# Gated projections with eight columns innermost: PSUM read with a step, SBUF written in order

## The chip, the core and the metric

The kernel runs on one core of a Trainium2 chip. The metric is device time in microseconds of one execution; the median of several runs counts. A profiled execution leaves a trace with the start and the duration of each engine's instructions. The engines are TensorE (PE; its weight loads are PEld), VectorE (DVE), ScalarE (ACT), GpSimd (POOL) and SyncE (SP), which issues DMAs. TensorE's results land in PSUM; the other memory on the core is SBUF.

## The reference, cut to what matters

Four layers run one after the other on an image batch of 4 x 128 x 128 x 128 floats, each as x + layer(group norm of x): a deformable convolution, a scan of 1-D convolutions over rows, a layer of summed messages, and a triangle layer. The change lies in the last one:

```python
xn = layer_norm(x, norm_g, norm_b)
left = xn @ left_w + left_b
right = xn @ right_w + right_b
left = left * jax.nn.sigmoid(xn @ lgate_w + lgate_b)
right = right * jax.nn.sigmoid(xn @ rgate_w + rgate_b)
out_gate = jax.nn.sigmoid(xn @ ogate_w + ogate_b)
out = jnp.einsum('bkjd,bkid->bijd', left, right)
out = layer_norm(out, onorm_g, onorm_b) * out_gate
return out @ to_out_w + to_out_b
```

## The kernel before, in words

The deformable convolution fills the span to about 3350 us and the scan to about 4100 us. The last two layers are one function, `message_and_triangle` (L1175). It takes the four images of the batch one at a time (b). One image lives in SBUF as X: 128 partitions by 128 columns by 128 floats.

For an image, `sums_of` builds X from the messages (products on TensorE at L1354, VectorE at L1365, squares on ScalarE at L1372). `turned` scales X (L1459), transposes it (L1469), copies it back (L1470) and counts its moments (L1476). `spread` applies the layer norm (L1494), transposes back (L1503, L1504), and computes the output gate (L1509, L1513), which it stores. These work on groups of 32 columns (g = 0 to 3), in blocks of 4 columns.

`projected` computes left and right with their gates for one quarter q of the 128 hidden channels (DQ = 32). A block covers QB = 8 columns. Eight matmuls (L1534, 16 records each block in the profile, as each matmul has two) fill a PSUM tile `proj_ps` of 8 columns by QC = 128 results: 32 of left, 32 of right, 32 of each gate. One sigmoid on ScalarE (L1538) turns the 64 gates of the 8 columns into the SBUF tile `work`. Two products on VectorE (L1540), one for left and one for right, multiply PSUM with `work` and write into L and R. L and R are laid out as partitions by channel by column, so that `triangle` (L1552, copied out by ScalarE at L1556) can take one channel's 128 columns as a matrix. PSUM holds each column's results side by side, so neighbouring columns of one channel lie 128 floats (512 bytes) apart in PSUM and side by side in L and R.

`proj_ps` has two buffers (pool `l3ps_q`), shared with `self_ps`; `work` has two too. A buffer of `proj_ps` is free for TensorE again when the second product, into R, has read it.

The order on each engine is written out by hand: `weave` interleaves lists of steps by their counts, and all five engines run in the order in which the steps were issued. For each image: five rounds (g = 0 to 4) that weave `turned` of group g+1, `spread` of group g and `projected` of quarters 0 and 1 for group g-1; the last of these rounds has projections alone. Then the triangle of quarter 0; then quarters 2 and 3, each woven with the triangle of the quarter before (two blocks of projections and one of triangle in turn), the last with small steps for the next image; then the triangle of quarter 3; then the moments of the result (L1567) and the output (`given`: L1595 and L1600 norm, L1610 transpose, L1612, L1613, L1620, L1624, L1627), woven with the next image's `sums_of` and `turned`.

Other lines that the prediction uses as measures: L509 (VectorE, 390 elements from PSUM and SBUF in order), L551 (VectorE, PSUM and SBUF in order), L507 and L530 (ScalarE copies from PSUM, L530 in runs of four floats), L1068 (ScalarE, PSUM in order), and the scan's VectorE lines, among them L1119 and L1127 (in order), L1128 (SBUF read at every third float) and L1145 (PSUM read and SBUF written at every third float).

Of the kernel before, what the change touches and what calls it, by code (L numbers as in the profile page):

```python
# [9 lines left out]
F32 = mybir.dt.float32  # L10
I32 = mybir.dt.int32
BF16 = mybir.dt.bfloat16
AF = mybir.ActivationFunctionType
ALU = mybir.AluOpType
# [4 lines left out]
P = 128  # L19
# [13 lines left out]
DQ = P // NQ  # L33
# [1141 lines left out]
def message_and_triangle(tc, c, x2T, x3d, gates, counted, w2, w3, out):  # L1175
# [3 lines left out]
    nc = tc.nc  # L1179
# [7 lines left out]
    QB = 8  # L1187
# [3 lines left out]
    with ExitStack() as ctx:  # L1191
# [25 lines left out]
        with tc.tile_pool(name="l3prep", bufs=1) as prep, tc.tile_pool(  # L1217
            name="l3ps_w", bufs=2, space=PSUM
# [38 lines left out]
        two = ctx.enter_context(tc.tile_pool(name="l3two", bufs=2))  # L1257
# [268 lines left out]
        def projected(b, q, j_from, j_to):  # L1526

            cols = slice(q * QC, (q + 1) * QC)
            ds = slice(q * DQ, (q + 1) * DQ)

            def block(j0):
                pp = ps_q.tile([P, QB, QC], F32, name="proj_ps", tag="ps_q")
                for j in range(QB):
                    nc.tensor.matmul(  # L1534
                        pp[:, j], lhsT=X[:, j0 + j, :], rhs=wcat[:, cols], start=True, stop=True
                    )
                sig = two.tile([P, QB, 2 * DQ], F32, name="work", tag="work")
                nc.scalar.activation(sig, pp[:, :, 2 * DQ :], AF.Sigmoid)  # L1538
                for n, to in enumerate((L[:, ds], R[q % 2])):
                    nc.vector.tensor_tensor(  # L1540
                        to[:, :, j0 : j0 + QB].rearrange("p d j -> p j d"),
                        pp[:, :, n * DQ : (n + 1) * DQ], sig[:, :, n * DQ : (n + 1) * DQ], ALU.mult,
                    )

            return [lambda j0=j0: block(j0) for j0 in range(j_from, j_to, QB)]
# [216 lines left out]
```

## Time and profile before

| | |
|---|---|
| median of 3 runs | 5691.27 us (5687.96 to 5703.16) |
| profiled execution | 5688.34 us, span 5686.6 us |
| busy: PE, PEld | 5214.1 us (92%), 4461.0 us (78%) |
| busy: DVE, ACT, POOL | 3277.2 us (58%), 2798.5 us (49%), 780.3 us (14%) |
| matmuls of L1534 | 4096 records, 488.9 us busy |
| sigmoids of L1538 | 256, 151.1 us |
| products of L1540 | 256 into L (154.6 us), 256 into R (152.7 us) |
| mean granted TensorE clock | 0.964 |

The projections run between 4219 and 5570 us of the span, in four stretches, one for each image. A group's row gives line, engine, operation, output and inputs, shapes and count; then the busy time in us and the mean duration of one in ns; then the idle time of the engine just before these instructions and what ended it. A row of the chain of waits gives start, duration and what was running; "issue" is time in which the engine waited for nothing that the profile shows. A mean duration is longer than the distance between two instructions of one engine that follow each other without a wait[...].

### The profile page before, as it was taken

To read this page: it belongs to the slowest core of one execution; us is meant where nothing else is said; L and a number is where in the kernel's file an instruction comes from. 1 tells how busy PE (TensorE), PEld (TensorE's weight loads), DVE (VectorE), ACT (ScalarE), POOL (GpSimd) and SP (SyncE) were. 2 spreads that over 40 slices of the span, in tenths; PEclk is the share of its full clock that TensorE was granted. 3 is DMA by queue.
4 is the path that set the end of the run, shared out by engine and by line. 5 is a ranking of instruction groups with operands and counts; after the bars stand their busy time and mean duration, and the time that the engine had idled before them with its cause. 6 is when DMAs were issued, how large, how long until landed. Compare 5 with 4: busy or idle time off the path is not lost. (4 is left out here: it accounts for less than half of the span.)

```text
span 5686.6 us, 112077 instructions
## 1 busy us (share of the span) xinstructions
PE 5214.1 (92%) x42401; PEld 4461.0 (78%) x42401; DVE 3277.2 (58%) x10323; ACT 2798.5 (49%) x5890; POOL 780.3 (14%) x674
## 2 busy tenths in 40 slices
PE   2899999999999999999999979999879788798897
PEld 1778888888888888888888879999848568577686
DVE  5544444554444544445433359999974764756756
ACT  1355554455554455555544423333264673764746
POOL 2021211001110011111000002222100200200202
PEclk9899999999999999999999989999989999999999
DMA  4555555556554555555443422222230531623515
GB/s 145 139 138 133 137 125 114 132 123 137 133 137 99 128 135 127 138 120 126 101 82 68 80 60 90 90 90 90 78 150 31 204 145 43 232 90 112 213 42 169
DMA packets 1132346, 671.45 MB, mean 118 GB/s; under 512 B 736461, under 2 KB 1002894, under 8 KB 1113366
## 3 DMA queue, kind: packets, MB, share of 16 engines
q1 hardware_dynamic: 1121650, 657.77, 43.6%
q8 instruction: 338, 5.54, 0.4%
q10 hardware_dynamic: 10148, 6.43, 0.4%
q14 instruction: 210, 1.72, 0.1%
HBM read 382.88 MB, written 281.11 MB: 117 GB/s over the span
## 5 line engine op out<-in xcount | busy, mean ns | idle before, releaser
L509 DVE TENSOR_TENSOR m<-ty,t_ps 120x390 f32<-120x390 f32 x1548 | 804.6, 557 | 1501.6 <-ACT ty L507 1500.4
L520 PEld LDWEIGHTS v_ps<-m,pixels 120*128 120x128 f32 x11352 | 1440.4, 194 | 86.0 <-issue 8.9
L520 PE MATMUL v_ps<-m,pixels 120*128 120x108 f32 (+1 forms) x11352 | 1466.3, 274 | 3.6 <-ACT v L530 3.5
L530 ACT COPY v<-v_ps 128x432 f32<-128x432 f32 x1376 | 718.9, 522 | 1275.8 <-PE v_ps L520 1272.8
L578 PE MATMUL conv_ps<-v,wdef 128*128 128x128 f32 (+2 forms) x5160 | 1304.0, 379 | 6.4 <-DVE x1c L551 5.9
L578 PEld LDWEIGHTS conv_ps<-v,wdef 128*128 128x128 f32 x5160 | 814.6, 193 | 255.8 <-issue 21.4
L507 ACT COPY ty<-t_ps 120x390 f32<-120x390 f32 x1560 | 688.1, 489 | 176.7 <-PE t_ps L497 169.2
L497 PE MATMUL t_ps<-places,spread 25*120 25x99 bf16 (+1 forms) x10836 | 520.4, 260 | 61.1 <-DVE m L509 36.5
L497 PEld LDWEIGHTS <-spread 25*120 25x120 bf16 x10896 | 339.3, 137 | 222.9 <-issue 121.5
L1534 PEld LDWEIGHTS proj_ps<-wcat,X 128*128 128x128 f32 x4096 | 480.2, 194 | 30.0 <-issue 29.0
L1534 PE MATMUL proj_ps<-wcat,X 128*128 128x128 f32 x4096 | 488.9, 278 | 1.7 <-DVE R L1540 0.4
L392 POOL TENSOR_TENSOR off<-off,koff 72x512 f32<-72x512 f32 x128 | 162.0, 1266 | 2295.5 <-DVE off L389 2202.7
L1540 DVE TENSOR_TENSOR L<-proj_ps,work 128x256 f32<-128x256 f32 x256 | 154.6, 604 | 384.8 <-ACT work L1538 384.8
L1068 ACT ACTIVATE rowT<-x1T_ps,t_x,s_x 128x128 f32<-128x128 f32 x512 | 192.7, 457 | 367.5 <-PE x1T_ps L1061 347.2
L1081 PE MATMUL m_ps<-carry,w 128*128 128x172 f32 x2286 | 361.7, 311 | 0.0
L1613 POOL TENSOR_TENSOR work<-work,gate 128x512 f32<-128x512 f32 x128 | 164.2, 1283 | 1417.6 <-ACT work L1612 1165.3
L1081 PEld LDWEIGHTS m_ps<-carry,w 128*128 128x128 f32 x2286 | 346.0, 188 | 0.0
L1148 POOL TENSOR_TENSOR sum_h<-sum_h,x2c 128x512 f32<-128x512 f32 x128 | 162.3, 1268 | 1166.7 <-DVE x2c L1145 1166.7
L1538 ACT ACTIVATE work<-proj_ps 128x512 f32<-128x512 f32 x256 | 151.1, 597 | 311.1 <-PE proj_ps L1534 311.1
L1624 PE MATMUL out_ps<-outw,work 128*128 128x128 f32 x1024 | 193.8, 292 | 34.1 <-POOL work L1613 33.5
L1354 PE MATMUL self_ps<-R,ws 128*128 128x512 f32 x256 | 157.6, 705 | 70.1 <-DVE X L1365 60.9
L1624 PEld LDWEIGHTS out_ps<-outw,work 128*128 128x128 f32 x1024 | 164.8, 203 | 46.8 <-POOL work L1613 46.8
(231 smaller groups left out, 6635.5 us busy)
## 6 DMA issues: line engine op xcount, KB each, us to landing
pixels<-tab SPq DMA_DIRECT2D x688, 123.8 KB
xin<-in_x_dram SPq DMA_DIRECT2D x56, 1024.0 KB
off<-parts SPq DMA_DIRECT2D x64, 891.0 KB
tab<-rows SPq DMA_DIRECT2D x384, 128.0 KB
places<-off SPq DMA_DIRECT2D x688, 55.7 KB
x<-x1c SPq DMA_DIRECT2D x32, 1024.0 KB
x1rows<-x SPq DMA_DIRECT2D x128, 256.0 KB
x2T<-x2c SPq DMA_DIRECT2D x128, 256.0 KB
```

Source lines behind the costliest of these rows:

```text
L497: nc.tensor.matmul(to, lhsT=spread[p0 : p0 + KROWS, ph, :], rhs=mov, start=True, stop=True,)
L507: nc.scalar.copy(ty[:, 0:n], tp[0:LANES, 0, 0:n])
L509: nc.vector.tensor_tensor(m, ty[:, 0:n].rearrange("p (r c) -> p r c", c=PADW), tx, ALU.mult)
L520: nc.tensor.matmul(vp[:, h * n : h * n + rows * w].rearrange("p (k c) -> p k c", c=w), lhsT=pix[0:LANES, xb, :], rhs=m[:, :, RX * xb : RX ...
L530: nc.scalar.copy(v[:, :, c0 : c0 + 4 * RX].rearrange("p k (h c) -> p k h c", c=RX), vp[:, 0 : 4 * n].rearrange("p (h k c) -> p k h c", h=4 ...
L578: nc.tensor.matmul(pc[:, at : at + r1 - r0, :], lhsT=wdef[:, 3 * ky + kx, :], rhs=v[:, k0 + kx, r0:r1, kx : kx + S], start=m == 0, stop=m ...
L1068: nc.scalar.activation(rt[:, b, :], px[:, b, :], AF.Identity, bias=t, scale=s)
L1081: nc.tensor.matmul(to, lhsT=wgt, rhs=src[:, :, at : at + n], start=i == 0, stop=i + 1 == len(todo),)
L1148: nc.gpsimd.tensor_tensor(sum_h, sum_h, x2c[:, :, i], add)
L1534: nc.tensor.matmul(pp[:, j], lhsT=X[:, j0 + j, :], rhs=wcat[:, cols], start=True, stop=True)
L1613: nc.gpsimd.tensor_tensor(a, a, gt, ALU.mult)
L1624: nc.tensor.matmul(po[:, j], lhsT=a[:, j], rhs=outw, start=False, stop=True)
```

## The change

Sigmoid and products go through the same elements in another order: channels outside, the eight columns innermost. `work` becomes channel by column in place of column by channel. The sigmoid and the products read PSUM with a step of 512 bytes between neighbours in the order of work; the products read `work` and write L and R in that order, in L and R as runs of eight floats. Before, they read PSUM in order and wrote L and R with a step of 512 bytes. Nothing else differs: the matmuls, the sizes of all tiles, the number of instructions and their order on each engine, and the waits are those of before.

```diff
-                sig = two.tile([P, QB, 2 * DQ], F32, name="work", tag="work")
-                nc.scalar.activation(sig, pp[:, :, 2 * DQ :], AF.Sigmoid)
+                sig = two.tile([P, 2 * DQ, QB], F32, name="work", tag="work")
+                nc.scalar.activation(
+                    sig, pp[:, :, 2 * DQ :].rearrange("p j n -> p n j"), AF.Sigmoid
+                )
                 for n, to in enumerate((L[:, ds], R[q % 2])):
+                    es = slice(n * DQ, (n + 1) * DQ)
                     nc.vector.tensor_tensor(
-                        to[:, :, j0 : j0 + QB].rearrange("p d j -> p j d"),
-                        pp[:, :, n * DQ : (n + 1) * DQ], sig[:, :, n * DQ : (n + 1) * DQ], ALU.mult,
+                        to[:, :, j0 : j0 + QB], pp[:, :, es].rearrange("p j d -> p d j"),
+                        sig[:, es], ALU.mult,
                     )
```

## The prediction

> **What bounds the kernel now.** I read the page first (busy times, costliest groups), then the groups by shape, then the timeline and the chain of waits over the stretch in which the projections run (4219 to 5570 us). By the page TensorE is busy 92% of the span, VectorE 58%, ScalarE 49%; what matters is where the two wait on the changed lines' chain. From the groups by shape (columns: count, then busy us and mean ns of one, then idle before):
>
> ```profile
> L1540 DVE TENSOR_TENSOR L<-proj_ps,work 128x256 f32<-128x256 f32 x256 | 154.6, 604 | 384.8 <-ACT work L1538 384.8
> ...
> L1567 DVE BATCH_NORM_STATS2 stats_o<-L 128x6 f32<-128x128 f32 x512 | 152.5, 361 | 33.0 <-ACT L L1556 33.0
> L1538 ACT ACTIVATE work<-proj_ps 128x512 f32<-128x512 f32 x256 | 151.1, 597 | 311.1 <-PE proj_ps L1534 311.1
> ...
> L1595 ACT ACTIVATE normed<-L,off_o,r_o 128x128 f32<-128x128 f32 x256 | 143.7, 612 | 3.1 <-DVE off_o L1446 3.1
> ...
> L1476 DVE BATCH_NORM_STATS2 stats_x<-X 128x6 f32<-128x128 f32 x512 | 110.6, 279 | 33.3 <-ACT X L1470 33.2
> ...
> L551 DVE SCALAR_TENSOR_TENSOR x1c<-conv_ps,xres 128x256 f32<-128x256 f32 x16 | 6.6, 415 | 0.0
> ```
>
> The reader is to see that a product of 256 elements that writes with a step of 512 bytes takes 604 ns, where a DVE operation of the same size with everything in order takes 415 (L551). The step costs 189 ns, 0.74 ns an element. Reading SBUF at that step costs much the same: 361 against 279 for 128 elements (L1567, L1476), 0.64 each. VectorE waits for the sigmoid before nearly every block, so sigmoid and products are one chain behind TensorE. Whether that chain sets the end differs by stage. Timeline where only projections are left (end of a batch's first two quarters):
>
> ```profile
> 4329.48 0.60 ACT L1538 ACTIVATE work<-proj_ps 128x512 f32<-128x512 f32 x1 [1.19 <-PE proj_ps L1534]
> ...
> 4330.11 0.61 DVE L1540 TENSOR_TENSOR L<-proj_ps,work 128x256 f32<-128x256 f32 x1 [0.75 <-ACT work L1538]
> 4330.56 0.60 DVE L1540 TENSOR_TENSOR R<-proj_ps,work 128x256 f32<-128x256 f32 x1
> ...
> 4331.61 0.60 ACT L1538 ACTIVATE work<-proj_ps 128x512 f32<-128x512 f32 x1 [1.54 <-PE proj_ps L1534]
> ```
>
> L and R start 0.45 us apart, so sigmoid to the end of R is 4329.48 to 4331.16: 1.68 us. There the chain shows two blocks every 3.92 us (pieces of 3.81 to 3.83 and 0.12 of issue), against 3.57 to 3.59 elsewhere: both PSUM buffers are held by the sigmoid and the products. In the stage with triangles a pair of blocks and a triangle take 4.47 us throughout; a buffer is free there at 4351.07 and wanted at 4351.81, so 0.74 us of slack hides the chain. In the stage that still turns X, the chain of waits is:
>
> ```profile
> 4238.10 3.59 PE proj_ps L1534 x32
> 4241.68 0.02 issue
> 4241.70 0.45 ACT work L1538
> 4242.15 0.04 issue
> 4242.20 0.40 ACT X L1459
> ```
>
> Only the sigmoid of the second block is on it; ScalarE's next work queues behind. One stage later (nothing left to turn), it goes on through VectorE:
>
> ```profile
> 4304.81 0.61 ACT work L1538
> 4305.41 0.02 issue
> 4305.44 0.59 DVE L L1540
> 4306.03 0.43 DVE R L1540
> 4306.46 0.18 DVE normed L1494
> 4306.64 0.14 issue
> 4306.78 1.01 PE back_ps L1503 x4
> ```
>
> Adding up all pieces of the chain from 4219 to 5570 us, L1538 is on it 53 times (29.6 us) and the products 80 times (40 of L, 40 of R; 39.7 us). The change can move only these and the 3.92 us loop.
>
> **The change part by part.** No instruction is added, removed or moved: every queue, SP's and POOL's included, holds the same instructions in the same order, with the same waits. Matmuls, DMAs, tile sizes and what L and R hold are the same. Three kinds of access change.
>
> Products, write side: runs of 8 floats (32 bytes) in place of single floats 512 bytes apart. Nearest row: ScalarE's square at L1372 reads SBUF in runs of four at that step, 512 elements in 721 ns, no dearer than L1459's 821 for 512 in order. I take the write as free: 604 goes to 415. The sigmoid's output and the products' second input stay in order: nothing.
>
> Products, read side: PSUM with a step of 512 bytes. No row has this step. Nearest is the scan's L1145, which reads PSUM and writes SBUF one float in three, 12 bytes apart, 172 elements in 378 ns; L1119, both in order, takes 336. So 42 ns for both sides together, 0.24 ns an element at most. Lower bound 0: reading SBUF at 12 bytes alone costs L1128 395 against L1127's 328 at 168 elements, 0.40 each, so the write can explain all of L1145. Upper bound, if PSUM behaves as SBUF: 0.64, which makes the product 415 + 164 = 579. I take 0, as L1145 is the only PSUM row with single floats and leaves little for the read. Below nothing is excluded: the read is in order now.
>
> Sigmoid, read side: the same step, 512 elements, ScalarE at 0.81 ns each (L1612's 769 for 512 less L1068's 457 for 128, over 384). The nearest ScalarE row is L530, PSUM in runs of four: 522 ns for 432, where L507's 489 for 390 plus 42 x 0.81 gives 523, so nothing; but it has no single floats. If L1145's whole 0.24 is the read, a float comes every 1.04 + 0.24 = 1.28 ns, and ScalarE pays 0.47 each, 0.24 us. If it is all the write, PSUM still only shows that it keeps VectorE's 1.04, and ScalarE pays at most 0.23 each, 0.12 us. The far end is the SBUF price: L1595 reads single floats at 512 bytes, 128 in 612 ns; L1068 does the same arithmetic from PSUM in order in 457, and SBUF as source adds 52 (821 of L1459 less 769 of L1612), so 103 ns for 128, 0.80 each, 0.41 us. I take 0.06 us, half of 0.12, and keep 0 to 0.41.
>
> Here a rule speaks against the change. The Trainium skill, "Advanced Engine Details and Errata", Memory Cachelines, says PSUM has lines of 8 bytes, wants every two consecutive elements to be neighbours, and warns that non-contiguous access slows matmuls; for SBUF it states a penalty for a new 16-byte line at every access. Charged on every float here at the SBUF rows' price, it makes the sigmoid 1.01 us and the product 579 ns. But L1145 at 12 bytes already meets a new 8-byte line at every float, and shows at most 0.24. By the row the sum is a gain, by the rule a loss (below). I go with the row.
>
> Sum. Back to back, the products now start 0.445 us apart; in order they should start 0.445 - 0.111 = 0.334 apart (L509's pairs: two of 390 in 1.03 us, 557 each, so 0.473 apart, 1.04 x 390 + 67, with 1.04 ns an element from L551's 549 for 384 and 415 for 256; for 256 this is 0.334). On the chain each pair is followed in VectorE's own queue, so it saves 2 x 0.11 = 0.22: 40 x 0.22 = 8.9 us. The loop: L's start to R's end shrinks from 1.05 to 0.334 + 0.415 = 0.75, by 0.30, and 3.92 falls to near TensorE's 3.59: 0.33 x 3 pairs x 4 batches = 4.0. Together 12.9. What is late next: in the stages with norm, ScalarE's copies and TensorE's gate product end soon after, at the end of a group ScalarE's two table loads (1.28 us each); I give a fifth back: 10.3. The sigmoid costs 53 x 0.06 = 3.2. Net 7.1 us. Products with triangles stay behind TensorE: zero, and that cover is 0.74 us, which would be gone only if sigmoid and products together grew by more.
>
> The profiled execution took 5688.3 (span 5686.6), the median of the runs is 5691.3, 2.9 higher. 5691.3 - 7.1 = 5684.2, so 5684.
>
> **The rivals.** *PSUM at SBUF's price* ends slower. Sigmoid +0.41 on 53 chain places: 21.8 us. Products 579 ns, but starting 0.334 + 0.164 = 0.498 apart, 0.05 more than now: 80 x 0.05 = 4.2. Loop +0.41 + 0.03 = 0.44, x 12 = 5.3. Sum 31: 5722. For it: the rule, and the SBUF rows agreeing on two engines (0.64 and 0.80). Against it: L1145. It decides once the sigmoid grows by 10.3/53 = 0.19 us with the products' gain kept, and passes 0.3% only at about 0.52 us, or 0.3 if the products gain nothing.
>
> *The step in between*, L1145's 42 ns all the read's: product 476 ns, starts 0.395 apart, 40 x 0.10 = 4 saved; loop 0.18 saved against 0.24 lost, near zero; sigmoid 53 x 0.24 = 12.7. Net 9 slower: 5700, within 0.3%.
>
> *Hidden anyway*: the products do get shorter, but a neighbour of equal length ends 0.1 us later, so nothing arrives: 5691. For it: the saving comes in pieces of 0.2 us in 40 places.
>
> *More than counted*: sigmoid free, nothing given back, and places where the chain passes just beside VectorE gain too: 12.9 plus a third, 17: 5674 or less.
>
> *Dearer yet*:[...] if that costs beyond 0.8 ns each, the 0.74 us with triangles goes as well: over 5730. No row shows it.
>
> **How the numbers follow.** About 0.3%, 17 us, is what a measurement of this kernel can tell from no change. Likeliest, 5684: 0.37, its own range 5676 to 5692. Hidden 0.10, in between 0.08: these three are within 0.3%, 0.55. SBUF's price 0.22 and dearer yet 0.08: slower, 0.30. More than counted: faster, 0.15. The range runs from 5672 to 5724: it takes in SBUF's price and leaves out the dearer case and half of the larger gain.
>
> **What would show each step.** L1540 at about 415 ns, pairs 0.33 apart: the write was the cost and the PSUM read is free; near 480 or 580 it is one of the rivals. L1538 at 600 to 700 is my case, about 1010 the rule's. The projection-only loop should fall from 3.92 to about 3.6 us a pair, the triangle stage keep 4.47. I am wrong if L1538 gains more than 0.2 us, or if products shorten as said while waits of TensorE for ScalarE (L1470, L1504, L1513) grow by the same amount.

## The result and the profile after

| | before | after |
|---|---|---|
| median of 5 runs | 5695.07 us (5687.96 to 5703.16) | 5665.21 us (5661.05 to 5667.66) |
| profiled execution, its span | 5688.34, 5686.6 us | 5661.53, 5659.8 us |
| DVE busy | 3277.2 us | 3206.4 us |
| mean granted TensorE clock | 0.964 | 0.966 |

The section ahead of the prediction had three runs of before; here it is five. The ratio is 0.9947, with a 95% interval of 0.9932 to 0.9961: 30 us less, beyond the 0.3% that the prediction named as measurable. 7 us had been forecast, and the time lies below the range.

The groups of instructions of the changed kernel (its sigmoid is still L1538, its products are L1543):

```profile
L1538 ACT ACTIVATE work<-proj_ps 128x512 f32<-128x512 f32 x256 | 151.1, 597 | 300.0 <-PE proj_ps L1534 300.0
...
L1543 DVE TENSOR_TENSOR L<-proj_ps,work 128x256 f32<-128x256 f32 x256 | 108.4, 424 | 425.8 <-ACT work L1538 425.8
...
L1543 DVE TENSOR_TENSOR R<-proj_ps,work 128x256 f32<-128x256 f32 x256 | 105.8, 413 | 0.0
```

The sigmoid takes 597 ns as before, to the nanosecond; the products take 424 and 413 where they took 604 and 596. So a PSUM read with a step of 512 bytes costs neither engine anything here. In the loop where only projections are left, the timeline of after shows:

```profile
4321.79 0.60 ACT L1538 ACTIVATE work<-proj_ps 128x512 f32<-128x512 f32 x1 [1.26 <-PE proj_ps L1534]
...
4324.20 0.42 DVE L1543 TENSOR_TENSOR L<-proj_ps,work 128x256 f32<-128x256 f32 x1 [1.03 <-ACT work L1538]
4324.55 0.41 DVE L1543 TENSOR_TENSOR R<-proj_ps,work 128x256 f32<-128x256 f32 x1
4325.43 0.60 ACT L1538 ACTIVATE work<-proj_ps 128x512 f32<-128x512 f32 x1 [1.26 <-PE proj_ps L1534]
```

L and R start 0.35 us apart (0.45 before), and a pair of blocks takes 3.64 us (3.92 before).

**Where the time came from.** Measured from the first projection to the last triangle of each image, the four stretches of projections take 859.2 us before and 831.6 after: 27.7 us less. Everything outside them took the same in this pair (4827.4 and 4828.2). The 27.7 us can be split, because many stages run at the full granted clock in both profiles, or in the experiments below:

| stage, at full clock | before | after | for four images |
|---|---|---|---|
| rounds 1 to 3 (turn, norm, projections), an image | 98.93 us | 96.03 us | -11.6 us |
| last round (projections alone), with the first triangle and the gap behind it | 22.95 | 21.78 | -4.7 |
| quarter 2 with triangles | 35.73 | 35.73 | 0 |
| quarter 3 with triangles and small steps, images 0 to 2 | 47.40 | 45.98 | -4.2 |
| quarter 3 of image 3, no small steps | 37.98 | 37.42 | -0.6 |

(Before's quarter 3 at full clock is from the fourth experiment, its third round from the tenth.) That is 21.1 us of shorter waits, called the direct part below. The other 6.6 us are stretches at half clock: in quarter 3, before lost 7.8 us to them (48.97, 52.06 and 48.96 us less 47.40 each) and after 1.5 (one of three took 47.52), and in the rounds both lost about 10.

**The half clock.** The trace records the clock that TensorE is granted; it is 1.00 or 0.50 of full speed throughout. The chain of waits in quarter 3 of image 0, first before, then after, goes from a pair of products through small steps on VectorE to the same small product of the next image and the 16 matmuls queued behind it:

```profile
4390.73 0.59 DVE L L1540
4391.32 0.43 DVE R L1540
4391.74 0.04 DVE m_x L1285
...
4392.40 0.38 PE gn_ps L1291 x2
4392.79 3.13 PE proj_ps L1534 x16
4395.92 1.28 PE tri_ps L1552 x8
```

```profile
4383.67 0.42 DVE L L1543
4384.09 0.33 DVE R L1543
4384.42 0.08 DVE m_x L1285
...
4385.12 0.38 PE gn_ps L1291 x2
4385.51 1.89 PE proj_ps L1534 x16
4387.40 0.89 PE tri_ps L1555 x8
```

The same 16 matmuls take 3.13 and 1.89 us. Windows of 3.41 us of before, aligned to its clock record (columns: us; busy time and count of PE, PEld, DVE, ACT, POOL; granted clock; DMA), show what went ahead of it:

```profile
4389.79:4393.20 3.41, 1.02 (x9) 0.83 (x9) 1.50 (x6) 0.60 (x1) 0.00 (x0) 1.00 0.00 0
4393.20:4396.61 3.41, 3.41 (x19) 3.41 (x18) 0.00 (x0) 0.60 (x1) 0.00 (x0) 0.50 0.00 0
```

In one slot TensorE was busy for 1.02 us, since it waited 2.39 us for VectorE ahead of L1291; in the next its clock was 0.50. After the change that wait is 2.17 us and falls into two slots, in which TensorE was busy for 2.75 and 1.91 us; the clock stayed full:

```profile
4380.20:4383.61 3.41, 2.75 (x25) 2.56 (x23) 0.76 (x2) 1.75 (x3) 0.00 (x0) 1.00 0.00 0
4383.61:4387.03 3.42, 1.91 (x17) 1.91 (x18) 1.30 (x6) 0.03 (x1) 0.00 (x0) 1.00 0.00 0
4387.03:4390.44 3.41, 3.41 (x33) 3.41 (x32) 0.75 (x2) 1.46 (x3) 0.00 (x0) 1.00 0.02 5
```

So at this place it is as much the position of the slots as the shorter wait that spared the half clock. What shorter waits do on the average is counted over all profiles further down.

### The profile page after: what moved, and what is told of

It reads as the page before. It is cut to its first block, busy times and chain, and to the rows that moved or that the text cites. A ratio compares the mean times of both kernels' runs of the same rounds, so it can differ in the third digit from the quotient of the medians.

```text
span 5659.8 us, 112077 instructions
## 1 busy us (share of the span) xinstructions
PE 5198.7 (92%) x42401; PEld 4450.7 (79%) x42401; DVE 3206.4 (57%) x10323; ACT 2796.7 (49%) x5890; POOL 780.2 (14%) x674
## 5 line engine op out<-in xcount | busy, mean ns | idle before, releaser
L1543 DVE TENSOR_TENSOR L<-proj_ps,work 128x256 f32<-128x256 f32 x256 | 108.4, 424 | 425.8 <-ACT work L1538 425.8
L1538 ACT ACTIVATE work<-proj_ps 128x512 f32<-128x512 f32 x256 | 151.1, 597 | 300.0 <-PE proj_ps L1534 300.0
```

## The experiments

Each ratio is to runs of the kernel before in the same set, on the same chip. Medians of before in the three sets (experiments 1 to 4, 5 to 8 and 9 to 11) are 5695.91, 5698.27 and 5695.30 us. My theory after the result was: (1) the sigmoid costs nothing; (2) more pairs of products are on the path than I had counted, above all where the chain of waits of before names ScalarE; (3) shorter waits of TensorE spare half-clock slots. Two rivals: that the gain is spread evenly over all pairs of products, and that the clock makes most of it and the direct part is about as small as forecast.

**1 to 3: one part of the work alone.** Each kernel chooses the order by quarter and keeps the old one elsewhere; the first has the condition shown, the second `q == 2`, the third `q == 3`:

```diff
+                if q < 2:
+                    sig = two.tile([P, 2 * DQ, QB], F32, name="work", tag="work")
...
+                else:
+                    sig = two.tile([P, QB, 2 * DQ], F32, name="work", tag="work")
...
```

Quarters 0 and 1 (the rounds):

> The new order in quarters 0 and 1 alone, the old one in 2 and 3. My theory now (the shorter products count wherever TensorE waits behind a pair in VectorE's queue, and shorter idle times of TensorE leave fewer stretches at half clock): 16 to 18 us faster than before, of which 4 in the projection-only loop. Rival, a gain that is spread evenly over the products (half of them are changed here): 15 us. Rival, only the 40 places counted on the chain of waits: about 10 us.

Measured: 5666.11 us, ratio 0.995 (0.9936 to 0.9964), 30 us less by the medians, which is more than the theory and both rivals expected; its profiled execution is 20 us below that of before, with 841.0 us in the projections, 18.2 less. The stages at full clock account for 16.3 (11.6 and 4.7, as in the table); the rest of the 30 us is not placed.

Quarter 2:

> The new order in quarter 2 alone, where triangles are woven in and TensorE hides the products. My theory: no change, within 3 us of before, the stage at 35.7 us for each image as before. Rival, a gain spread evenly over the products (a quarter is changed): 7.5 us faster.

Measured: 5698.32 us, ratio 1.0003 (0.9995 to 1.001). Quarter 2 took 35.73 us in all four images, as before and after. A gain spread evenly over all pairs would have shown here; that rival falls. With triangles the products are hidden, as predicted.

Quarter 3:

> The new order in quarter 3 alone, where small steps for the next image are woven in. My theory: about 11 us faster, some 5 to 6 of it fewer stretches at half clock behind the waits for those steps. Rival, spread evenly: 7.5 us. Rival, the counted chain alone (12 pairs at 0.22): 3 us.

Measured: 5686.43 us, ratio 0.9986 (0.9977 to 0.9996), 8 to 9.5 us less. In the profile quarter 3 took 47.84, 49.42, 47.90 and 37.72 us, 5.1 less in all than before. The chain of before has five pairs there in each of the first three images, and one pair in the last: at the forecast 0.22 us that is 3.5 (the expectation had counted 12). The 5 to 6 us that the theory expected from the clock did not come: four slots ran at half clock in these quarters, five in before's. By the medians the three parts add up to 39 us, the whole change to 30; their intervals are wide enough for that, so the stages and not these medians say what each part is worth.

**4: before, with spare matmuls in the waits of quarter 3.** Three products of 256 columns go ahead of each of the three small products of the next image (L1291, L1310, L1322), into PSUM columns that nobody reads. Nothing else of before is changed:

```diff
+        def busy(to, n):
+            for _ in range(n):
+                nc.tensor.matmul(
+                    to[:, 256:512], lhsT=c.gmean, rhs=wcat[:, 0:256], start=True, stop=True
+                )
...
-                v["ps"] = small_ps([P, 1], "gn_ps4")
+                wide = small_ps([P, 512], "gn_ps4")
+                v["ps"] = wide[:, 0:1]
+                if b:
+                    busy(wide, 3)
```

> The kernel before, with TensorE kept busy in its three waits for the next image's small steps in quarter 3 (three spare products of 256 columns each, about 1.3 us, into columns of PSUM that nobody reads; images 1 to 3). The products on VectorE are the old ones. My theory, in which half clock follows from TensorE's idle time in the 3.4 us before: the half-clock stretches of quarter 3 go away (5 in the profile before), 5 to 8 us faster. Rival, in which the half-clock stretches have another cause: no change, or up to 4 us slower by the spare products.

Measured: 5680.21 us, ratio 0.9974 (0.9967 to 0.9982), 15 us less, above what was expected. Quarter 3 of image 1, windows of before and then of this kernel:

```profile
4760.20:4812.30 52.10, 43.27 (x335) 42.17 (x333) 20.78 (x53) 17.47 (x28) 0.00 (x0) 0.90 0.06 19
```

```profile
4750.10:4797.60 47.50, 42.52 (x353) 40.47 (x352) 20.80 (x53) 17.47 (x28) 0.00 (x0) 1.00 0.07 23
```

18 more matmul records, VectorE and ScalarE with the same work, and 4.6 us less: the granted clock went from 0.90 to 1.00. Over three images quarter 3 lost 7.8 us with its products at 605 and 597 ns. So the clock's part is shown without any shorter product. The rest of the 15 us is not placed: the profile differs by 11 us before the first projection, where the two kernels are the same and this one happened to spend 225 us at half clock, before 246.

**5: after, with the sigmoid in two instructions**, so that L could start when its half of the gates is there:

```diff
-                nc.scalar.activation(
-                    sig, pp[:, :, 2 * DQ :].rearrange("p j n -> p n j"), AF.Sigmoid
-                )
+                for n in range(2):
+                    gs = slice((2 + n) * DQ, (3 + n) * DQ)
+                    nc.scalar.activation(
+                        sig[:, n * DQ : (n + 1) * DQ],
+                        pp[:, :, gs].rearrange("p j n -> p n j"), AF.Sigmoid,
+                    )
```

> The changed kernel with the sigmoid in two instructions, the 256 gates of left first, then those of right. ScalarE's work grows by about 0.05 to 0.1 us a block, but VectorE's first product can start about 0.2 us earlier. If in the rounds that still turn X TensorE waits for VectorE's norm behind the products (my reading of the changed kernel's trace), these rounds get about 0.2 us shorter each, quarter 3 about 1 us an image, and the whole 10 to 15 us faster than the changed kernel. Rival, the recorded chain, in which ScalarE's queue behind the sigmoid holds those rounds: they get 0.05 to 0.1 us longer, and the whole is 0 to 3 us from the changed kernel.

Measured: 5679.48 us, ratio 0.9965 (0.9953 to 0.9978), 10 to 15 us slower than after (0.9939 to 0.9947) by the ratios. A miss. Its timeline shows why:

```profile
4230.41 0.66 ACT L1540 ACTIVATE work<-proj_ps 128x256 f32<-128x256 f32 x2 [0.76 <-PE proj_ps L1534]
4231.10 0.42 DVE L1546 TENSOR_TENSOR L<-proj_ps,work 128x256 f32<-128x256 f32 x1 [1.97 <-ACT work L1540]
```

The second half ends at 4231.07, and L starts 0.03 us later: it waited for both. The trace's semaphores say why: the first half raises none, the second raises the one that L waits for, in all 256 pairs. So the edit did not do what it was for; it only made the sigmoid 0.06 us longer. All of it arrived: rounds 1 to 3 took 0.06 us more a pair of blocks (8.03 to 8.09, 9.82 to 9.88), the last loop 3.70 for 3.64. That is the price of a sigmoid of 0.66 us which my prediction had feared. And quarter 3 took 49.33, 49.56 and 51.07 us, with seven slots at half clock where after has one. The rounds came out as the rival had said, but since L never started earlier, this run cannot tell the two readings apart.

**6: after, with each product in two of 16 channels**, which lengthens VectorE's part and nothing else:

```diff
+                    for h in range(2):
+                        hs = slice(h * DQ // 2, (h + 1) * DQ // 2)
+                        es = slice(n * DQ + h * DQ // 2, n * DQ + (h + 1) * DQ // 2)
...
-                            to[:, :, j0 : j0 + QB], pp[:, :, es].rearrange("p j d -> p d j"),
+                            to[:, hs, j0 : j0 + QB], pp[:, :, es].rearrange("p j d -> p d j"),
```

> The changed kernel with each product in two instructions of 16 channels: same access, but four starts of about 0.2 us each in place of two of 0.334, so a pair holds VectorE about 0.13 us longer, more than half of the 0.22 that the change took away. My theory: 10 to 16 us slower than the changed kernel, each clean round 0.13 us longer per pair on VectorE's path. Rival, only the 40 counted places and the loop: 6 to 7 us slower.

Measured: 5674.05 us, ratio 0.9959 (0.9943 to 0.9975), 7 to 11 us slower than after by the ratios, 9.8 us by the projections of the profiles: between the two forecasts. The single pairs tell more. The last loop went from 3.64 to 3.77 us a pair, by 0.13. The pairs of rounds which the chain of before had put down to ScalarE's gate (L1513) grew by the same 0.13: 8.03 to 8.16 and 9.82 to 9.95. VectorE sets the end there too, and now the chain of waits itself, at the place where before's went down ScalarE (shown in the next section), names VectorE's queue all the way:

```profile
4243.43 0.61 ACT work L1538
...
4244.06 0.49 DVE L L1545 x2
4244.54 0.40 DVE R L1545 x2
4244.94 0.78 DVE stats_x L1476 x4
4245.72 0.26 DVE normed L1494
...
4246.12 1.00 PE back_ps L1503 x4
```

Quarter 3 took 46.42 us three times, with no half-clock slot although its waits are longer than after's: whether a wait costs a slot also depends on where the slots begin.

**7: the products of after with the sigmoid of before.** PSUM is read with a step and L and R are written in order, but `work` stays column by column, so that the products read it with a step of 256 bytes in SBUF:

```diff
-                sig = two.tile([P, 2 * DQ, QB], F32, name="work", tag="work")
-                nc.scalar.activation(
-                    sig, pp[:, :, 2 * DQ :].rearrange("p j n -> p n j"), AF.Sigmoid
-                )
+                sig = two.tile([P, QB, 2 * DQ], F32, name="work", tag="work")
+                nc.scalar.activation(sig, pp[:, :, 2 * DQ :], AF.Sigmoid)
...
-                        sig[:, es], ALU.mult,
+                        sig[:, :, es].rearrange("p j d -> p d j"), ALU.mult,
```

> One half of the change alone: the products write L and R in order and read PSUM with the step, but the sigmoid keeps its old order, so the products read their second input from SBUF with a step of 256 bytes. If a stepped SBUF read costs 0.64 ns an element beside the PSUM read, the product takes about 580 ns and the time is that of before or up to 12 us slower. Rival, the step costs on the write alone: 415 to 425 ns and the time of the changed kernel.

Measured: 5712.32 us, ratio 1.0029 (1.0016 to 1.0042), 14 us slower than before by the medians, a little over the 12 expected at most. From its groups of instructions:

```profile
L1541 DVE TENSOR_TENSOR L<-proj_ps,work 128x256 f32<-128x256 f32 x256 | 152.5, 596 | 389.5 <-ACT work L1538 389.5
L1538 ACT ACTIVATE work<-proj_ps 128x512 f32<-128x512 f32 x256 | 151.2, 597 | 321.4 <-PE proj_ps L1534 245.2 <-DVE R L1541 76.2
L1541 DVE TENSOR_TENSOR R<-proj_ps,work 128x256 f32<-128x256 f32 x256 | 150.7, 589 | 0.0
```

The products are back at 596 and 589 ns: by its duration a product pays as much for the step on the reading side of SBUF as on the writing side; in PSUM it pays nothing. The gain of the change hangs on the sigmoid's new order. The products are 8 ns shorter than before's, and yet rounds and loop are longer (8.39 for 8.25, 3.99 for 3.93 us). The timeline of the loop shows why a mean duration is not enough:

```profile
4333.46 0.60 DVE L1541 TENSOR_TENSOR L<-proj_ps,work 128x256 f32<-128x256 f32 x1 [1.09 <-ACT work L1538]
4333.98 0.59 DVE L1541 TENSOR_TENSOR R<-proj_ps,work 128x256 f32<-128x256 f32 x1
```

R starts 0.52 us after L; over all pairs the median is 0.51 us, against 0.45 before and 0.34 after. A product thus holds VectorE 0.17 us longer with the stepped read and 0.11 us longer with the stepped write. The 0.06 us between them is the loop's loss, and two of them most of the 0.14 in the rounds. Half-clock time in the projections is 88.7 us, against 47.8.

**8: after, with the spare matmuls of the fourth kernel.**

> The changed kernel with the same spare products on TensorE in quarter 3. Fewer half-clock stretches are left there to remove (one in the changed kernel's profile): 1 to 5 us faster than the changed kernel, quarter 3 at 46.0 us in each of the first three images. Rival, in which the filled waits are not what lowers the clock: no difference, or up to 4 us slower.

Measured: 5659.53 us, ratio 0.9931 (0.9916 to 0.9947). That is 5 to 9 us below after by the ratios (1 to 5 were expected), but the intervals overlap. Quarter 3 took 45.98, 45.99 and 45.98 us without a half-clock slot. With the same matmuls added on both sides, quarter 3 differs from the fourth kernel by 1.41 us an image: the direct part alone.

**9 to 11: after once more, and before and after with spare matmuls in the rounds too.** The last two kernels add to the fourth's edit, ahead of the first two transposes and the first transpose back of g = 3, into PSUM that these then overwrite:

```diff
+                if g == 3 and k < 2:
+                    nc.tensor.matmul(
+                        pt[:, k:], lhsT=c.gmean, rhs=wcat[:, 0 : (JB - k) * S],
+                        start=True, stop=True,
+                    )
...
+                if g == 3 and k == 0:
+                    for _ in range(2):
+                        nc.tensor.matmul(
+                            pb, lhsT=c.gmean, rhs=wcat[:, 0:512], start=True, stop=True
+                        )
```

> The changed kernel once more, beside the next two on the same chip: 30 us faster than before as at first; anything from 22 to 36, since the half-clock stretches fall differently in every execution.

> The kernel before with spare products on TensorE in all its long waits among the projections: the three of quarter 3, and the starts of the last two rounds that still turn or norm (0.65 to 1.7 us each, into PSUM columns that the real product overwrites). My theory: hardly a half-clock stretch is left between the first and the last projection of an image; 12 to 18 us faster than before, with the products still at 604 ns. Rival: no difference from the kernel with quarter 3 filled alone.

> The same spare products in the changed kernel. With half clock gone from both, only the direct part of the change is left between this and the filled kernel before: by the rounds that were free of half clock in both profiles 0.85 + 1.05 + 1.0 + 1.06 + 0.1 us an image, and 1.4 in quarter 3 of three images: 21 us in all. Rival, the 40 counted places and the loop: 13 us. Against the changed kernel it should gain 5 to 10 us.

Measured: after again 5661.51 us, ratio 0.9939 (0.9926 to 0.9952). Before with spare matmuls 5674.08, ratio 0.9967 (0.9957 to 0.9978). After with them 5646.41 (5637.71 to 5656.91), ratio 0.9917 (0.9902 to 0.9932): 49 us below before, the fastest of all, and 15 below after (5.4 in the projections of the two profiles), where 5 to 10 were expected. Half-clock time in the projections falls from 47.8 to 3.4 us for before and from 27.3 to 6.8 for after, with the products of before still at 604 ns. The times alone do not tell the filled kernel before from the fourth (0.9967 and 0.9974, overlapping intervals); in the profiles its projections are 8.4 us shorter.

With the clock nearly out of it, the two differ by 17.6 us in the projections of their profiles (843.4 and 825.8), by 19.3 when what half clock still cost in single rounds (1.7 and 3.4 us) is taken off, and by 20.9 when what the spare matmuls themselves add to the second round (0.17 and 0.59 us an image) goes too: theory 2 expected 21, the rival 13. By the medians the difference is 28 us, and the two intervals leave about 10 us on either side. So the direct part is well shown by the stages, and the total of direct part and clock only to within some 10 us: medians of runs give 30 where the two profiles give 27.

## Why the prediction was wrong, step by step

**Products at 415 ns with a free PSUM read: right** (424 and 413), and of the range for the stepped read, 0 to 0.64 ns an element, the low end holds: 424 against 415 leaves at most 0.04. The rule weighed against it, PSUM lines of 8 bytes that want two neighbouring elements (the Trainium skill, "Advanced Engine Details and Errata", Memory Cachelines), cost nothing on these two engines here: by it the sum was a loss. L1145 had spoken against it; that its 42 ns are all the writing side's is now likely, but a step of 12 bytes was not tried.

**"I take 0.06 us, half of 0.12"** for the sigmoid: wrong in size. It grew by 0.000 us. So the 3.2 us for it never came. Had it grown by 0.06, that much would have arrived in each pair of the rounds and of the last loop, as the fifth experiment shows.

**The last loop, 4.0 us: right.** 3.92 went to 3.64, 4.3 us in all; another 0.4 came from the start of quarter 2.

**"Products with triangles stay behind TensorE: zero": right**, to 0.00 us in four images.

**"40 x 0.22 = 8.9 us": the step that failed most.** It took the pairs that the chain of waits names for all the pairs that count. The rounds hold 24 of the 40 pairs and were to give 5.3 us; they gave 11.6. Seven of these pairs lie in the first two rounds, worth 1.5 us by the forecast: these two rounds gave 7.6. The third holds 16 and gave 4.0 for 3.5, so there the count was near; one lies in the last round. Quarter 3 holds the other 16 and was to give 3.5; it gave 4.8. Two things were too small. A pair on the chain saves not 0.22 us but 0.26: in quarter 3, L's start to the next instruction of VectorE on the chain (L1285) goes from 1.01 us to 0.75 (the chains of waits above). And the chain of waits names one releaser where two end together. The timeline of before, in the first round, at the place where the chain passes from the sigmoid through X and the gate to back_ps:

```profile
4243.84 0.62 ACT L1513 ACTIVATE gate<-gate_ps 128x512 f32<-128x512 f32 x1
4244.00 1.10 DVE L1494 TENSOR_SCALAR normed<-X,mu_x,r_x 128x127 f32<-128x127 f32 x4
...
4244.48 1.00 PE L1503 MATMUL back_ps<-ident,normed 128*128 128x128 f32 x4 [0.30 <-ACT gate L1513]
```

The chain blames the gate, which ended 0.02 us earlier. The same place after:

```profile
4240.84 1.10 DVE L1494 TENSOR_SCALAR normed<-X,mu_x,r_x 128x127 f32<-128x127 f32 x4
4240.90 0.62 ACT L1513 ACTIVATE gate<-gate_ps 128x512 f32<-128x512 f32 x1
4241.32 1.00 PE L1503 MATMUL back_ps<-ident,normed 128*128 128x128 f32 x4
```

Now back_ps starts 0.20 us before the gate's end, so it does not need that gate. What it keeps in both is its distance to VectorE's norm: 0.48 us after its start. And the norm stands in VectorE's queue behind the moments and the two products. So the chain walked down ScalarE, while VectorE with its products ended at the same time and was the one that counted. Rounds with such places gained 0.21 to 0.22 us a pair (8.25 to 8.03, 10.04 to 9.82), which is the very sum that I had made for the pairs I counted; the sixth experiment confirms it in the other direction.

**"I give a fifth back": wrong.** Nothing was given back that can be seen: the first round, with four pairs, became 0.85 us shorter, 0.21 a pair on the average, of the 0.22 forecast, and the loop 0.28 of 0.30.

**What the sum did not have: the granted clock.** It is 6.6 of the profile's 27.7 us. So the forecast was 5.3 in the rounds, 3.5 in quarter 3 and 4.0 in the loop, less 2.6 and 3.2, some 7; the two profiles show 11.6, 4.8 and 4.7, with nothing taken off, and 6.6 from the clock. The prediction looked at TensorE's waits only for their length. The fourth experiment shows what they cost besides. That shorter waits bring fewer slots at half clock shows over several profiles, not in one pair. In quarter 3 without spare matmuls the old order has 5, 5 and 7 such slots (before and experiments 1 and 2), the new one 1, 4 and 1 (after, 3 and 9); in rounds 1 to 3 the old order has 9, 11, 8 and 9 (before, 2, 3 and 4), the new one 7, 6, 4 and 7 (after, 1, 8 and 9). They differ from image to image of one profile (one, three and one in quarter 3 of before), so the 6.6 us hold for this pair of profiles alone.

Of the rivals, *more than counted* had the right direction and most of the mechanism (sigmoid free, nothing given back, places beside the chain gain too), but at 17 us was still below the 21 measured, and knew nothing of the clock. The range ended at 5672 and left out half of that case.

## What to carry over

When data must change order between PSUM and SBUF, put the step on the PSUM side and measure one group: here it was free there, and in SBUF, read or written, it made an instruction 0.64 to 0.74 ns an element longer. Measure the distance between the starts of two instructions as well as their duration. Before counting pieces of a chain of waits, look in the timeline at what else ended within some hundredths of a microsecond of the releaser that it names, and follow both queues. And where TensorE waits 2 us again and again, look at the granted clock behind each wait: a shorter wait, or spare matmuls in it, can be worth more than the wait's own length.

## What the runs showed of the hardware

**Half clock comes after partial idleness.** In the traces every stretch of the granted clock's record within the span is a multiple of 3.41 us, so it is read here in slots of that length. In the 13 profiles of this case, between the first and the last projection, the slots that follow one in which TensorE was busy for under 40% ran at half clock in 238 of 238 cases; after 40 to 45% in 63 of 73; after 45 to 50% in 42 of 80; after 50 to 60% in 62 of 319; after 60 to 90% in 89 of 1131; after over 90% in 5 of 3264. The Trainium skill, "TensorE: Matmul & The Clock Gate", HAM oscillation, gives as rule that no idle gap be over about 3.4 us; here no wait of TensorE inside the projections was longer than 2.9 us, and waits of 2.2 to 2.7 us were enough when they fell mostly into one slot. By that rule the clock would have had no part in this change. The slots do not start with the kernel: the same waits of quarter 3 cost one slot in two images of before's profile and three in another.

**Most of the spread between profiles lies ahead of the projections.** There all kernels are the same, and yet the first projection starts between 4208.0 us (the fourth experiment, 225.3 us at half clock until then) and 4233.1 us (the eighth, 266.2 us). Over the 13 profiles each further microsecond at half clock goes with about 0.54 us of time. That the clock is the cause there too was not tried by itself. This is why the stages are compared, and not one whole profile with another.

**A stepped PSUM read is free for ScalarE and VectorE** at 512 bytes, single floats: 597 ns for both orders of the sigmoid, and 424 and 413 ns for the products where L551, with everything in order, takes 415.

**The fifth experiment says nothing of PSUM.** L waited for the second half of the sigmoid because the program signals VectorE only there. Whether L could run beside the second half, which reads the same PSUM tile, stays open.
